# Reading places to registers per stretch instead of per group in a graph network's count stage

## The chip, the cores and the metric

The kernel runs on one core of a Trainium2 chip. Its time is device time in microseconds (us) for one launch. The unchanged kernel took 1696.02 us (median of three runs, 1693.77 to 1696.36).

A core has five engines with a queue of instructions each: PE (matrix multiply; PEld is its weight load), DVE and ACT (elementwise, vector and scalar engine), POOL (elementwise and general) and SP (here an issuer of DMAs). An engine's queue also executes instructions that compute nothing, such as a register load; in the profile such time is marked with a q (ACTq, POOLq, DVEq) and doesn't count as busy.

## What is computed

A graph has 6250 nodes with 128 features and 200,000 edges, sorted by their target `dst`; each edge has a source `src` and 128 features of its own. The reference, cut to what matters:

```python
h = relu(layernorm(x))
agg_src  = segment_sum(h[src], dst, 6250)
agg_edge = segment_sum(edge_attr, dst, 6250)
x = x + relu(concat([h, agg_src, agg_edge]) @ W.T + b)
h = relu(layernorm(x))
for Wl, bl, Wr in two layers:                      # mean over a node's edges
    agg = segment_sum(h[src], dst, 6250) / maximum(degree, 1)
    h = relu(agg @ Wl + bl + h @ Wr)
x = x + h
```

## The kernel before

**Two phases.** The sum over edges of `h[src]` is turned into a matrix product with a matrix of edge counts (how many edges go from source s to target d). The first phase, up to some 720 us of the profiled span, builds these counts in DRAM (`counts_d`) and adds up the edge features (`aggE`). The second (from L657 on) multiplies the counts with the nodes' features, once per layer (L753); the change doesn't touch it.

**Groups, tiles, windows.** The edges come in 196 groups of 1024, a group as U = 8 tiles of 128. For each group DVE writes one-hots by comparing an index with `iota`: `sp` (the source's row, 8 x 128, L567) and `sq` (target and source column within a window, L570), and weighs one of them (L572 or L574). For n = 1 a third one, `sc` (L584), carries edges over the border between windows. PE multiplies `sp` with `sq` into the PSUM tile `pu` (L597, L609; two windows per tile, three buffers). A window takes n tiles: 4 in the first 28 groups, 2 in the next 56, 1 in the last 112. ACT copies a window's counts from `pu` into an SBUF tile, the ring, at a place that depends on the data.

**The places.** `at_i` holds a window's place in the ring for every tile, `first_i` the first node of every group; both are int32 on one partition, computed on the chip. An engine that uses such a place reads it to a register first. `group_values` (L431) makes one instruction (TENSOR_LOAD, L433) that reads several values, `value` (L427) one that reads one (L428). In every group ACT reads its windows' places (L576: 2, 4 or 8 values for n = 4, 2, 1; they are n apart in `at_i`) and, for n > 1, POOL reads the same again (L578). For n = 1 ACT alone puts a window into the ring (L624). For n > 1 ACT copies the first columns, which overlap the window before, to `fore` (L619), POOL adds them to the ring (L627), and ACT puts the rest (L629).

**Stretches and rings.** Consecutive groups share one ring for a stretch: 14 groups in the first region, then 7, 4, 3, 2, and 2 or 3 for n = 1; 70 stretches in all, 44 of them with n = 1. At a stretch's end POOL reads `first_i` and issues the DMA that writes the ring to `counts_d` (L646, L647), between 0.3 and 1.8 MB by the width of its region. For n > 1 POOL begins a stretch by copying the seam from the ring before (L561, L562). There are three rings in turn, so a ring is free again when the write of three stretches earlier has landed.

**Edge features and first layer beside it.** `edge_sums` (L477) loads a group's features (512 KB, SP's queue, five buffers), has DVE write a one-hot `hot` (L484), has PE multiply (L493), and then reads the group's first node to a DVE register (L496) and adds the result into `aggE` there (L498). It is a generator: L635 lets it emit its 8 matmuls spread between those of the counts, by the shares of L546, and each is tied behind the last count matmul. Every third group also emits one block of the first layer (L641): statistics, a transpose through `pu` (L387), the product with the weights (L394), ACT's copies hT (L389) and feats (L395).

**Order.** The program's order is what the loops emit; the framework's scheduler may move an instruction ahead of earlier ones of its engine that are not ready in its own model, and the order per engine is then fixed. The one-hots `sp`, `sq` and `sc` come from the pool `hots` with two buffers each (L410); a third group's one-hots have to wait until PE has read the first's.

Of the kernel before, what the change touches and what calls it, by code (L numbers as in the profile page):

```python
# [19 lines left out]
ET = mybir.EngineType  # L20
# [5 lines left out]
U = 8  # L26
# [10 lines left out]
NONE = 2047.0  # L37
RUN = 14
XB = 4


REGIONS = (
# [20 lines left out]
def kernel(ctx: ExitStack, tc: tile.TileContext, x, srcl, dstl, edge, w0t, b0, w1l, b1, w1r, w2l, b2, w2r, out):  # L63
# [11 lines left out]
    nc = tc.nc  # L75
    N = x.shape[0]
# [3 lines left out]
    NJ = -(-NB // NC3)  # L80
    G = srcl.shape[1] // U
# [62 lines left out]
    aggE = keep.tile([P, NP + WINMAX], F32, name="aggE")  # L144
    c_early = keep.tile([P, P, NJ], I32, name="c_early")

    build = ExitStack()
# [5 lines left out]
    at_i = lists.tile([1, GC * U], I32, name="at_i")  # L153
    first_i = lists.tile([1, G], I32, name="first_i")
# [43 lines left out]
    for key, t in [*pick.items(), *pick_l.items()]:  # L198
        n = key if isinstance(key, int) else key[0]
# [110 lines left out]
    while si < NS:  # L310
        g0, k = stretches[si][:2]
# [95 lines left out]


    rings = build.enter_context(tc.tile_pool(name="rings", bufs=1))
    hots = build.enter_context(tc.tile_pool(name="hots", bufs=2))  # L410
    edges = build.enter_context(tc.tile_pool(name="edges", bufs=5))

    ring_of = [rings.tile([P, SWMAX * NJ], I32, name=f"ring{i}") for i in (2, 1)]
# [13 lines left out]
    def value(ap, engine, most):  # L427
        return nc.values_load(  # L428
            ap, engines=[engine], min_val=0, max_val=most, skip_runtime_bounds_check_because="clamped on the chip"
        )  # L430

    def group_values(ap, engine, most):
        _, values = nc.values_load_multi_w_load_instructions(  # L433
            ap, engines=[engine], min_val=0, max_val=most, skip_runtime_bounds_check_because="clamped on the chip"
        )
        return values
# [17 lines left out]
    def carries():  # L454
# [19 lines left out]
            carry[:, 0:1], flat_q[:, T1 - 2 : T1 - 1], pu[:, 0:1].unsqueeze(2).to_broadcast([P, 1, 2]), op=ALU.subtract  # L474
        )

    def edge_sums(g):  # L477

        win = win_of(g)
        e = edges.tile([P, U, D], F32, name="edge_t")  # L480
        at_e = min(g * EG, E - EG)
        nc.sync.dma_start(e, edge[at_e : at_e + EG, :].rearrange("(p u) f -> p u f", u=U))
        hot = padded[g % len(padded)]
        nc.vector.tensor_tensor(  # L484
            hot[:, : U * win].rearrange("p (u w) -> p u w", w=win),
            iota[:, :win].unsqueeze(1).to_broadcast([P, U, win]),
            rel[:, g, :].unsqueeze(2).to_broadcast([P, U, win]),
            op=ALU.is_equal,
        )
        ps = bpsum.tile([P, 512], F32, name="pe", bufs=2)  # L490
        for u in range(U):
            behind = yield
            mm = nc.tensor.matmul(ps[:, :P], e[:, u, :], hot[:, u * win : u * win + P], start=u == 0, stop=u == U - 1)  # L493
            if behind is not None:
                tc.add_manual_dep(mm.ins, behind.name, IN_ORDER, reason="in turn with the counts")
        base = value(first_i[0:1, g : g + 1], ET.DVE, N - 1)  # L496
        to = aggE[:, bass.ds(base, win)]
        nc.vector.tensor_tensor(to, to, ps[:, :win], op=ALU.add)  # L498

    def all_edge_sums():  # L500
# [54 lines left out]
    for si, (g0, ng, n, w, k, sw, win) in enumerate(stretches):  # L555
        nq = NJ * w
        ring = ring_of[si % 3]
        if si == NS - 1:
            nc.gpsimd.memset(ring[:, : sw * NJ].bitcast(F32), 0.0)
        if before is not None and n > 1:  # L560
            v = value(seam_i[0:1, si : si + 1], ET.Pool, (SWMAX - 1) * NJ)  # L561
            nc.gpsimd.tensor_copy(ring[:, :NJ], before[:, bass.ds(v, NJ)])  # L562
        for g in range(g0, g0 + ng):
            if g == RUN:
                carries()
            sp = hots.tile([P, U, P], BF16, name="sp")
            onehots(sp, p_e[:, g], U, P)  # L567
            even = nq + nq % 2
            sq = hots.tile([P, U, NQ + NQ % 2], BF16, name="sq")
            onehots(sq[:, :, :even], q_e[:, g], U, even)  # L570
            if nq < P and n > 1:
                weigh(sq[:, :, :even], g, even)  # L572
            else:
                weigh(sp, g, P)  # L574
            places = at_i[0:1, g * U : (g + 1) * U : n]
            to_put = group_values(places, ET.Activation, (sw - w) * NJ)  # L576
            if n > 1:
                to_add = group_values(places, ET.Pool, (sw - w) * NJ)  # L578
            else:

                of_first = 2 if g == G1 else 1
                sc = hots.tile([P, U + 1, NJ + NJ % 2], BF16, name="sc")
                c0 = g * U - T1 + 1
                onehots(  # L584
                    sc[:, 2 - of_first : U + 1], carry[:, c0 + 1 - of_first : c0 + U], U + of_first - 1, NJ + NJ % 2
                )
            live = [t for t in range(0, U, n) if g < G - 1 or (t + n) * P > unused]
            many = 2 if nq <= 512 else 1
            for j in range(0, len(live), many):
                units = live[j : j + many]  # L590
                pu = bpsum.tile([P, 2 * 512], F32, name="pu", bufs=3)
                for i, t0 in enumerate(units):
                    for t in range(t0, t0 + n):
                        c = i * 512
                        while c < i * 512 + nq:
                            z = min(c // 512 * 512 + 512, i * 512 + nq)
                            mm = nc.tensor.matmul(  # L597
                                pu[:, c:z],
                                sp[:, t, :],
                                sq[:, t, c - i * 512 : z - i * 512],  # L600
                                start=t == t0,
                                stop=t == t0 + n - 1 and (n > 1 or c > i * 512),
                            )
                            c = z
                    if n == 1:

                        slot = t0 + 1 if t0 != live[0] else 1
                        for j0, (sp_b, t) in enumerate(last_tiles):
                            mm = nc.tensor.matmul(  # L609
                                pu[:, i * 512 : i * 512 + NJ],  # L610
                                sp_b[:, t, :],
                                sc[:, slot + 1 - len(last_tiles) + j0, :NJ],
                                start=False,
                                stop=j0 == len(last_tiles) - 1,
                            )
                    last_tiles = [(sp, t) for t in range(t0, t0 + n)]
                if n > 1:
                    fore = hots.tile([P, 2, NJ], I32, name="fore", bufs=8)
                    nc.scalar.copy(  # L619
                        fore[:, : len(units), :], pu.rearrange("p (i c) -> p i c", c=512)[:, : len(units), :NJ]  # L620
                    )
                for i, t0 in enumerate(units):
                    if n == 1:
                        nc.scalar.copy(ring[:, bass.ds(to_put[t0], nq)], pu[:, i * 512 : i * 512 + nq])  # L624
                        continue
                    to = ring[:, bass.ds(to_add[t0 // n], NJ)]
                    add = nc.gpsimd.tensor_tensor(to, to, fore[:, i, :], op=ALU.add)  # L627
                    tc.add_to_no_dep_group(f"add{si}", add.ins)
                    put = nc.scalar.copy(  # L629
                        ring[:, bass.ds(to_put[t0 // n] + NJ, nq - NJ)], pu[:, i * 512 + NJ : i * 512 + nq]  # L630
                    )

                    tc.declare_no_dep(put.ins, group=f"add{si}", reason="a later window's other nodes stand behind it")
                spent += share(n) * len(units) / len(live)
                sum_edges(min(int(spent / shares * GU + 0.5), GU), counted)  # L635
                counted = mm.ins

            if len(writes) > 1 or block == NB and writes:
                writes.pop(0)()
            if g % 3 == 1 and block < NB:  # L640
                writes.append(first_layer(block))  # L641
                block += 1
        if si == 0:
            begin = 0
        else:
            begin = value(first_i[0:1, g0 : g0 + 1], ET.Pool, N - 1) * NJ  # L646
        write = nc.gpsimd.dma_start(counts_d[:, bass.ds(begin, sw * NJ)], ring[:, : sw * NJ])  # L647
        if si >= EARLY:
            tc.declare_no_dep(write.ins, group="early", reason="it begins behind the first block, or all is computed again")
        if si == EARLY - 1:  # L650
            tc.add_to_no_dep_group("early", load_counts(nc.gpsimd, c_early, 0).ins)
        before = ring
# [547 lines left out]
```

## Time and profile before

| | before |
|---|---|
| median of the runs shown | 1696.02 us |
| the profiled execution | 1698.32 us |
| its span | 1696.7 us |
| granted TensorE clock | 0.977 |
| PE, DVE, ACT, POOL busy | 92%, 77%, 51%, 18% |
| register loads: ACT L433, POOL L433 | 196, 84 |
| register loads: DVE L428 | 196 |
| ring writes (POOL, L647) | 70 |

The table's counts and shares come from one profiled execution. A line of a group of instructions names the source line, the engine, the operation and out<-in; a line of waits reads "who waited <- for whom: us in total, times, longest us". The chain of waits goes back from the last instruction to what released each step and gives shares by line; it can be asked for a window of time alone. The windows give each engine's busy time in a stretch of the span.

### The profile page before, as it was taken

To read this page: it belongs to the slowest core of one execution; us is meant where nothing else is said; L and a number is where in the kernel's file an instruction comes from. 1 tells how busy PE (TensorE), PEld (TensorE's weight loads), DVE (VectorE), ACT (ScalarE), POOL (GpSimd) and SP (SyncE) were. 2 spreads that over 40 slices of the span, in tenths; PEclk is the share of its full clock that TensorE was granted. 3 is DMA by queue.
4 is the path that set the end of the run, shared out by engine and by line. 5 is a ranking of instruction groups with operands and counts; after the bars stand their busy time and mean duration, and the time that the engine had idled before them with its cause. 6 is when DMAs were issued, how large, how long until landed. Compare 5 with 4: busy or idle time off the path is not lost.

```text
span 1696.7 us, 38957 instructions
## 1 busy us (share of the span) xinstructions
PE 1561.9 (92%) x13563; PEld 1506.6 (89%) x13563; DVE 1303.3 (77%) x2810; ACT 869.3 (51%) x2183; POOL 297.3 (18%) x657
## 2 busy tenths in 40 slices
PE   5998887889988888779999999899999999999998
PEld 5897777778878877669999999899999999999998
DVE  9887776678878778777777777888676777777775
ACT  3434443566766666655555555554444453444442
POOL 2534555200000000131211222201000020000000
PEclk9999998999999999979999999999999999999999
DMA  1877766678877788766666567455555556666662
GB/s 61 261 255 252 246 224 220 237 259 278 284 274 273 276 294 311 270 230 209 199 204 214 199 222 227 169 185 199 196 189 202 185 174 206 228 219 220 221 223 97
DMA packets 122572, 377.02 MB, mean 222 GB/s; under 512 B 15249, under 2 KB 67151, under 8 KB 99712
## 3 DMA queue, kind: packets, MB, share of 16 engines
q1 hardware_dynamic: 98676, 289.00, 51.2%
q0 software_dynamic: 15088, 80.80, 12.9%
q10 hardware_dynamic: 8604, 4.66, 0.9%
q8 instruction: 109, 1.79, 0.4%
q14 instruction: 95, 0.78, 0.2%
HBM read 289.94 MB, written 84.45 MB: 221 GB/s over the span
## 4 chain that ended last, share of the span: by engine, by line
PE 69%; ACT 11%; issue 7%; ACTq 4%; DVE 4%; DMA 3%; POOL 1%; POOLq 1%; DVEq 0%
PE ps L753 50%; PE pe L493 10%; ACT ring L624 9%; ACTq L433 4%; PE pu L597 3%; DMA counts_d<-ring 3%; PE pz L394 2%; PE pu L394 1%; PE pt L296 1%; PE pt L387 1%; PE ps L751 1%; ACT ring L629 0%; DVE sq L440 0%; DVE sp L440 0%; DVE w_n L247 0%
## 5 line engine op out<-in xcount | busy, mean ns | idle before, releaser
L753 PE MATMUL ps<-terms,wide 128*128 128x256 f32 (+1 forms) x7203 | 939.7, 290 | 20.0 <-DVE terms L706 13.0
L753 PEld LDWEIGHTS ps<-terms,wide 128*128 128x128 f32 x7203 | 905.5, 198 | 26.4 <-issue 13.2
L697 DVE CAST wide<-c 128x1024 fp32r<-128x1024 uint8 (+1 forms) x584 | 524.2, 907 | 145.8 <-PE ps L753 145.3
L697 ACT CAST wide<-c 128x1024 fp32r<-128x1024 uint8 x292 | 361.5, 1238 | 294.3 <-PE ps L753 233.5
L493 PE MATMUL pe<-hot,edge_t 128*128 128x128 f32 x3136 | 490.2, 293 | 8.8 <-DVE aggE L498 5.0
L493 PEld LDWEIGHTS pe<-hot,edge_t 128*128 128x128 f32 x3136 | 406.2, 196 | 15.2 <-DVE aggE L498 6.2
L624 ACT CAST ring<-pu 128x170 f32 (+6 forms) x891 | 256.1, 289 | 135.3 <-PE pu L609 57.4
L597 PE MATMUL pu<-sq,sp 128*128 128x136 bf16 (+8 forms) x1563 | 200.3, 225 | 61.5 <-ACT ring L624 37.3
L597 PEld LDWEIGHTS <-sp 128*128 128x128 bf16 x1563 | 135.6, 100 | 32.4 <-issue 25.8
L440 DVE TENSOR_TENSOR sp<-iota,p_e 128x1024 bf16<-128x1024 f16 x196 | 134.9, 688 | 37.5 <-PE pu L597 20.6
L440 DVE TENSOR_TENSOR sq<-iota,q_e 128x1088 bf16<-128x1088 f16 (+8 forms) x196 | 141.8, 723 | 13.2 <-PE pu L609 12.1
L398 POOL DMA_DIRECT2D r_d<-r x98 | 53.4, 545 | 506.4 <-DVE r L397 484.3
L609 PEld LDWEIGHTS <-sp 128*128 128x128 bf16 x892 | 80.7, 97 | 57.9 <-issue 51.6
L627 POOL TENSOR_TENSOR ring<-ring,fore 128x17 int32 x280 | 101.8, 363 | 116.0 <-ACT fore L619 37.8
L609 PE MATMUL pu<-sc,sp 128*128 128x17 bf16 x892 | 112.5, 173 | 0.0
L629 ACT CAST ring<-pu 128x119 f32 (+5 forms) x280 | 65.8, 245 | 75.8 <-issue 34.1
L647 POOL DMA_DIRECT2D counts_d<-ring x70 | 37.9, 542 | 374.5 <-ACT ring L624 310.4
L450 DVE TENSOR_TENSOR sp<-sp,w_e 128x1024 bf16<-128x1024 bf16 x140 | 95.9, 685 | 0.0
L484 DVE TENSOR_TENSOR hot<-iota,rel 128x64 f32<-128x64 f16 (+13 forms) x196 | 94.2, 484 | 0.0
L498 DVE TENSOR_TENSOR aggE<-aggE,pe 128x8 f32 (+13 forms) x196 | 37.7, 193 | 56.7 <-PE pe L493 38.2
L397 DVE TENSOR_TENSOR r<-pz,b_sb 128x128 f32<-128x128 f32 x98 | 28.0, 286 | 67.1 <-ACT feats L395 66.7
L772 DVE TENSOR_REDUCE y<-ps 128x128 f32<-128x256 f32 x147 | 60.9, 415 | 8.4 <-PE ps L753 8.4
(167 smaller groups left out, 961.1 us busy)
## 6 DMA issues: line engine op xcount, KB each, us to landing
c<-counts_d SPq DMA_DIRECT2D x146, 1088.0 KB, 5.0
edge_t<-in_edge SPq DMA_DIRECT2D x196, 512.0 KB, 4.6
own<-r_d SPq DMA_DIRECT2D x147, 64.0 KB, 1.8
counts_d<-ring POOLq DMA_DIRECT2D x5, 1785.0 KB, 7.9
counts_d<-ring POOLq DMA_DIRECT2D x5, 1598.0 KB, 8.2
counts_d<-ring POOLq DMA_DIRECT2D x5, 1462.0 KB, 8.0
counts_d<-ring POOLq DMA_DIRECT2D x5, 1377.0 KB, 6.2
r_d<-r POOLq DMA_DIRECT2D x98, 64.0 KB, 2.1
```

Of the source, the lines that this page charges most:

```text
L433: _, values = nc.values_load_multi_w_load_instructions(ap, engines=[engine], min_val=0, max_val=most, skip_runtime_bounds_check_because="c ...
L440: nc.vector.tensor_tensor(to.rearrange("p t (c two) -> p t c two", two=2), iota[:, :m].rearrange("p (c two) -> p c two", two=2).unsqueeze( ...
L450: nc.vector.tensor_tensor(pairs, pairs, w_e[:, g].bitcast(BF16).unsqueeze(2).to_broadcast([P, U, m // 2, 2]), op=ALU.mult)
L484: nc.vector.tensor_tensor(hot[:, : U * win].rearrange("p (u w) -> p u w", w=win), iota[:, :win].unsqueeze(1).to_broadcast([P, U, win]), re ...
L493: mm = nc.tensor.matmul(ps[:, :P], e[:, u, :], hot[:, u * win : u * win + P], start=u == 0, stop=u == U - 1)
L597: mm = nc.tensor.matmul(pu[:, c:z], sp[:, t, :], sq[:, t, c - i * 512 : z - i * 512], start=t == t0, stop=t == t0 + n - 1 and (n > 1 or c ...
L609: mm = nc.tensor.matmul(pu[:, i * 512 : i * 512 + NJ], sp_b[:, t, :], sc[:, slot + 1 - len(last_tiles) + j0, :NJ], start=False, stop=j0 == ...
L624: nc.scalar.copy(ring[:, bass.ds(to_put[t0], nq)], pu[:, i * 512 : i * 512 + nq])
L627: add = nc.gpsimd.tensor_tensor(to, to, fore[:, i, :], op=ALU.add)
L629: put = nc.scalar.copy(ring[:, bass.ds(to_put[t0 // n] + NJ, nq - NJ)], pu[:, i * 512 + NJ : i * 512 + nq])
L697: copy(t[:, : p1 - p0], two)
L753: dense = nc.tensor.matmul(ps[:, :m], wide[i, q][:, p, :, two], terms[:, s, :m], start=s == 0, stop=s == NB - 1)
```

## The change

The register reads are taken out of the group: ACT and POOL read all places of a stretch in its first group, in one instruction each; DVE reads the first nodes of 14 groups at once. The uses index into the longer lists. The pool `hots` gets three buffers. The diff, whole:

```diff
@@ -37,6 +37,7 @@
 NONE = 2047.0
 RUN = 14
 XB = 4
+FIRSTS = 14
@@ -407,7 +408,7 @@
-    hots = build.enter_context(tc.tile_pool(name="hots", bufs=2))
+    hots = build.enter_context(tc.tile_pool(name="hots", bufs=3))
@@ -474,6 +475,8 @@
+    bases = []
+
     def edge_sums(g):
@@ -493,8 +496,9 @@
-        base = value(first_i[0:1, g : g + 1], ET.DVE, N - 1)
-        to = aggE[:, bass.ds(base, win)]
+        if g % FIRSTS == 0:
+            bases[:] = group_values(first_i[0:1, g : min(g + FIRSTS, G)], ET.DVE, N - 1)
+        to = aggE[:, bass.ds(bases[g % FIRSTS], win)]
         nc.vector.tensor_tensor(to, to, ps[:, :win], op=ALU.add)
@@ -572,11 +576,12 @@
-            places = at_i[0:1, g * U : (g + 1) * U : n]
-            to_put = group_values(places, ET.Activation, (sw - w) * NJ)
-            if n > 1:
-                to_add = group_values(places, ET.Pool, (sw - w) * NJ)
-            else:
+            if g == g0:
+                places = at_i[0:1, g0 * U : (g0 + ng) * U : n]
+                to_put = group_values(places, ET.Activation, (sw - w) * NJ)
+                if n > 1:
+                    to_add = group_values(places, ET.Pool, (sw - w) * NJ)
+            if n == 1:
@@ -621,13 +626,13 @@
-                        nc.scalar.copy(ring[:, bass.ds(to_put[t0], nq)], pu[:, i * 512 : i * 512 + nq])
+                        nc.scalar.copy(ring[:, bass.ds(to_put[(g - g0) * U + t0], nq)], pu[:, i * 512 : i * 512 + nq])
                         continue
-                    to = ring[:, bass.ds(to_add[t0 // n], NJ)]
+                    to = ring[:, bass.ds(to_add[((g - g0) * U + t0) // n], NJ)]
...
-                        ring[:, bass.ds(to_put[t0 // n] + NJ, nq - NJ)], pu[:, i * 512 + NJ : i * 512 + nq]
+                        ring[:, bass.ds(to_put[((g - g0) * U + t0) // n] + NJ, nq - NJ)], pu[:, i * 512 + NJ : i * 512 + nq]
```

## The prediction, made before the result

> **What bounds the kernel now.** I read the page's chain first, then busy time by stage, then the chain of each stage, then every register load.
>
> ```profile
> PE 69%; ACT 11%; issue 7%; ACTq 4%; DVE 4%; DMA 3%; POOL 1%; POOLq 1%; DVEq 0%
> PE ps L753 50%; PE pe L493 10%; ACT ring L624 9%; ACTq L433 4%; PE pu L597 3%; DMA counts_d<-ring 3%; PE pz L394 2%; PE pu L394 1%; PE pt L296 1%; PE pt L387 1%; PE ps L751 1%; ACT ring L629 0%; DVE sq L440 0%; DVE sp L440 0%; DVE w_n L247 0%
> ```
>
> ACTq L433 is ACT's instruction queue standing at a register load: 4% of 1696.7 us can be touched at all. The layers (L753, from 720 us on) hold none of the edited lines. Busy time by stage (the first group takes n = 4 tiles per window until 112 us, n = 2 until 311, n = 1 until 720):
>
> ```profile
> core 0: us, PE busy (x) PEld busy (x) DVE busy (x) ACT busy (x) POOL busy (x), PEclk, DMA share, GB/s
> 44.00:112.00 68.00, 64.86 (x647) 61.87 (x645) 59.62 (x187) 26.72 (x118) 34.21 (x64) 0.95 0.82 263
> 112.00:190.00 78.00, 70.10 (x676) 64.77 (x676) 63.48 (x200) 36.05 (x198) 37.67 (x104) 1.00 0.77 253
> 190.00:311.00 121.00, 97.10 (x836) 89.52 (x835) 86.24 (x222) 48.07 (x244) 62.80 (x160) 0.92 0.68 227
> 311.00:720.00 409.00, 353.35 (x3592) 326.06 (x3592) 321.44 (x732) 267.43 (x954) 29.36 (x56) 0.98 0.79 277
> ```
>
> PE leaves 56 us idle for n = 1 and 24 us in the second half of n = 2; that is where time is to be had. The chain of those two stages, n = 1 first:
>
> ```profile
> by line: ACT ring L624 37.8%; PE pe L493 18.0%; ACTq L433 11.8%; issue 11.6%; PE pu L597 6.5%; DMA counts_d<-ring 5.5%; PE pu L394 1.5%; ACT h L376 1.2%; PE pu L609 0.9%; DVE sq L440 0.8%; ACTq L624 0.8%; DMA x_c<-in_x 0.8%; DVE sp L440 0.6
> ...
> by line: issue 31.3%; DMA counts_d<-ring 18.1%; PE pe L493 14.0%; ACTq L433 5.9%; POOLq L433 5.2%; PE pu L597 5.0%; POOL ring L627 4.5%; ACT ring L629 3.7%; POOLq L428 3.5%; POOLq L627 2.6%; ACT fore L619 1.7%; PE pu L394 1.0%; POOLq L647 0
> ```
>
> For n = 1, ACT's loads are 11.8% of 409 us = 48 us of the chain. PE's waits agree:
>
> ```profile
> PE pu L597 <- ACT ring L624: 37.3, 64, 2.4
> PE pe L493 <- DVE aggE L498: 5.0, 6, 2.4
> ```
>
> In the second half of n = 2, POOL has no room. One stretch of it:
>
> ```profile
> 240.39 0.56 POOL L647 DMA_DIRECT2D counts_d<-ring  x1 [0.80 <-ACT ring L629]
> 240.95 0.73 POOL L562 COPY ring<-ring 128x17 int32 x1
> 242.71 1.42 POOL L627 TENSOR_TENSOR ring<-ring,fore 128x17 int32 x4 [1.03 <-issue]
> 244.92 1.93 POOL L627 TENSOR_TENSOR ring<-ring,fore 128x17 int32 x4 [0.79 <-ACT ring L629]
> 247.35 0.56 POOL L647 DMA_DIRECT2D counts_d<-ring  x1 [0.49 <-ACT ring L629]
> ```
>
> The 1.03 and the 0.79 are the tails of at_i loads (1.62 and 1.08 us); the rest of the 7 us is POOL's own work.
>
> **What a load costs.** Durations are minimum/median/maximum in ns: windows 80-98 us (two values, 4 apart), 190-305 us (four values, 2 apart), 340-720 us (eight in a row).
>
> ```profile
> L433 POOLq TENSOR_LOAD <-at_i x7: 495/497/502, 81.3 to 95.9; - x7
> L433 ACTq TENSOR_LOAD <-at_i x7: 472/475/666, 82.6 to 96.8; - x7
> ...
> L433 ACTq TENSOR_LOAD <-at_i x31: 882/899/2895, 190.1 to 302.3; - x31
> L433 POOLq TENSOR_LOAD <-at_i x31: 940/1162/2540, 193.1 to 303.9; - x31
> ...
> L433 ACTq TENSOR_LOAD <-at_i x103: 537/550/2937, 342.2 to 714.0; - x103
> ```
>
> Values that lie apart cost ACT (0.888-0.471)/2 = 0.21 us each over 0.055 fixed, POOL 0.22 over 0.05: batching them saves almost nothing. Eight in a row cost 0.55, hence 0.49 over the same fixed part. The maxima matter more. Put beside the issues of ring writes (L647), load by load, slow ones begin about 1 to 3.5 us after an issue: DVE's one-value load takes 0.30 outside, 0.7 to 1.6 inside; ACT's eight take 0.55 and mostly 1.7 to 2.5. Each stretch has one such slow load in its middle or second group; at 573 us a write is issued, at 575.5 ACT's load takes 2.26, and 1.96 of that is on the chain.
>
> **The change, part by part.** ACT, n = 1 (112 groups in 24 stretches of three and 20 of two). The 110 loads that start there add up to 112.7 us; unslowed they would be 110 x 0.55 = 60. After it: 24 values in a row cost between 1.1 (one value 0.30, each further one (0.55-0.30)/7) and 3 x 0.55 = 1.65; I take 0.055 + 3 x 0.49 = 1.53, nearest to the row of eight, and 1.04 for 16. Sum 24 x 1.53 + 20 x 1.04 = 58 us. They stand at the stretch's start. There, in 30 of the 44, ACT now loads from 0.3 us before its last put ends; POOL issues 0.3 after that end; so 1.53 us end 0.9 after the issue, just short of the slow time. In the other 14 first-layer work comes first and part of the load falls into it. The slow eight lose 1.6 over two halves, 0.8 a step; I add a quarter of a step to the 30 and one and a half to the 14, 23 us. So 81 replaces 113: -32 of load time. Of the 113, 48 were on the chain (0.43 per us): -14. Each load is also followed by some 0.2 us until the next put, against 0.03 between puts; 66 loads fewer x 0.18 x 0.43 = -5. Together **-19**, between -5 and -45 (all of the chain's 48 less a little). Queued behind the longer load are the puts of L624 and hT and feats of the first layer; PE waits for them, but has three pu buffers of some 0.73 us (two windows and their edge matmuls) ahead, which hide 1.5 us. Where that cover is gone each load costs its 1.2 us.
>
> One rule speaks against this: the Trainium skill (Perfetto Trace Analysis, Identifying the Most-Contended Engine) calls the engine with the highest occupancy the one to optimize, and takes ScalarE's occupancy as a fair measure. ACT is busy 267 of 409 us, PE 353: by the rule ACT has 35% to spare and its loads are worth 0, the whole change +12 from POOL and DVE below, 1708. The row ACTq L433 says 48 us, because a load holds ACT's queue without counting as busy. I follow the row.
>
> POOL, n = 2. In 190-311 us 16 stretches have 32 loads, 44.8 us: the first, issued 0.4 us after the ring write, averages 1.76, the second 1.04. One load of eight values then costs at least 1.83 unslowed plus the first's present excess, 2.6; at most twice the slowest seen, 5.1. I take 2 x 1.76 = 3.5, each half slowed like the first now: +0.7 per stretch. Some 0.25 of the second load lay under POOL's last add and is now exposed; one handover less gives 0.15 back. +0.8 x 16 x 0.8 (POOL waits for ACT about a fifth of this stage) = **+10** (0 to +25). Behind it stand the adds (L627), the next ring write and so, over the ring's reuse, ACT's puts. In 112-190 us nine longer stretches by the same 0.8, at half weight since PE is 90% busy: **+4** (0 to +10). A second rule would price this otherwise: Runtime: NRT & Kernel Launch, breakdown of the preamble, gives a TENSOR_LOAD some 1.3 us as one round trip to HBM for a few words. Per instruction, POOL would gain 16 x 1.3; but these loads read SBUF, and the rows go by value, two 0.50, four 0.94. I take the rows.
>
> ACT, n = 2: 112 values apart in 112-190 us are 24 us plus slowing, about 30, against 28.8 now: 0 (-6 to +6); there is slack, for ACT runs ahead of POOL. n = 4: one load of 28 values (5.9 us on ACT, 6.3 on POOL) at 45-53 us, before ACT's first count is there at 55; then 3.0 us twice, under three pu buffers of about 2 us each: 0 (to +4).
>
> DVE: 196 loads, 101 us, become 14 loads of 14 values, from 0.9 (by the row of eight) to 4.3 (one by one); I take 0.9. The aggE add and the one-hots behind it queue after it. PE waited for that add only 5.0 us: **-2** (-5 to +4).
>
> Third one-hot buffer: DVE waits 25 us for PE to free sp or sq for n = 1 and 18 for n = 2, but PE hardly ever waits for one-hots, so DVE was merely early: 0; down to -5, or up to +5 if one-hots are now put ahead of aggE adds.
>
> Sum: -19 + 10 + 4 - 2 = -7 on an execution of 1698.3 us (span 1696.7 and 1.6 around it), 1691 there. That execution lies 2.3 above the median of 1696.0, so on the median **1689**.
>
> **Rivals.** *POOL hidden, ACT fully freed:* the n = 1 chain loses nearly all 48 us, POOL's extra is absorbed: 1696 - 40 = 1656. For it: PE's idle 56 us; against: POOL has no gaps in n = 2. *Loads are priced by value wherever they stand* (the batch doesn't save what it says): POOL's +14 and -14 on ACT and DVE: 1696. For it: two and four apart are proportional. *Slower: the ring write catches ACT's batch.* If ACT's load of 24 starts over 0.1 us later relative to the issue, as in the 14 stretches now, it runs through the slow time; three steps at +0.8 give 1.5 + 2.3 = 3.9 against 3.2 for three loads before, of which 0.6 more was hidden: with the handovers +0.9 per stretch of three, +0.8 of two, 38 us, about half on the chain, +20, and POOL's +14: 1730. Against it: 30 of 44 stretches start their load in time.
>
> **Numbers.** Likeliest case 0.50, own range 1676 to 1696; all freed 0.16; cancelled 0.12; slower 0.22, from 1700 to 1735. The range, 1658 to 1712, leaves out the fastest part of the second and the slowest of the fourth. A measurement can tell about 0.2%, 3.4 us, that is below 1692.6 or above 1699.4: faster 0.41 + 0.16 = 0.57, same 0.09 + 0.09 = 0.18, slower 0.03 + 0.22 = 0.25.
>
> **What would show it.** ACT loads for n = 1: 44, mean 1.5 to 2.1; ACTq L433 at some 7% of that stage and its length about 390; POOL loads above 3 us and 190-311 longer by about 10. I am wrong if ACT's batches exceed 2.5 us, if POOL's stay under 2.6, or if PE waits for DVE's adds.

## The result and the profile after

The changed kernel took 1720.97 us (median of four runs, 1715.31 to 1725.43) against 1695.9 for the one before (four runs beside it): ratio 1.0149, interval 1.0113 to 1.0184. The forecast was 1689, with a range of 1658 to 1712. The change is slower by 25 us.

In the profiled execution (span 1723.8 us) the layers start 24.4 us later than before (753.1 against 728.7) and then take 970.7 us against 968.0. So nearly all of the loss lies in the count phase. The page's chain after, by engine and by line:

```profile
PE 70%; issue 9%; DVE 5%; ACT 5%; ACTq 4%; DMA 3%; POOLq 1%; POOL 1%; DVEq 0%
PE ps L758 49%; PE pe L496 12%; ACTq L434 4%; ACT ring L629 3%; PE pu L602 3%; DMA counts_d<-ring 3%; PE pz L395 2%; DVE sp L441 1%; PE pt L297 1%; PE pu L395 1%; PE pt L388 1%; DVE sq L441 1%; ACT ring L634 1%; PE ps L756 1%; POOLq L434 1%
```

ACTq still has 4% though its reads fell from 196 to 70: fewer reads, as much time on the chain. L434 is now the read of several values on every engine. To compare stages I cut them where the last ring write of a stage is issued: n = 4, the n = 2 stretches of four and three groups, the n = 2 stretches of two groups, n = 1. Before, they took 71.2, 94.5, 105.9 and 404.4 us. The windows of the first two stages before, and of all four after:

```profile
44.00:115.20 71.20, 68.06 (x682) 65.03 (x680) 62.21 (x195) 28.61 (x126) 34.64 (x66) 0.95 0.81 261
115.20:209.70 94.50, 81.45 (x779) 75.20 (x778) 74.96 (x233) 40.84 (x227) 47.19 (x131) 0.99 0.76 252
...
44.00:134.10 90.10, 75.59 (x707) 70.62 (x704) 63.98 (x221) 28.10 (x138) 33.92 (x67) 0.90 0.64 216
134.10:249.90 115.80, 88.63 (x708) 79.65 (x706) 69.12 (x199) 35.68 (x202) 42.71 (x130) 0.89 0.54 184
249.90:361.60 111.70, 86.94 (x776) 81.33 (x775) 76.90 (x197) 47.92 (x229) 52.76 (x140) 0.95 0.67 228
361.60:744.40 382.80, 346.58 (x3566) 324.84 (x3565) 313.57 (x724) 266.46 (x942) 27.21 (x48) 0.98 0.82 293
```

The columns are as in the prediction. The stages changed by +18.9, +21.3, +5.8 and -21.6. A stage's length from a single execution wavers: in runs that left all reads of a stage as they were, n = 4 took 71.2 to 73.4 us, the longer n = 2 stretches 92.5 to 96.1, and n = 1 took 392.5 to 404.4. So the first two losses are far outside the noise, and the gain for n = 1 is somewhere between 10 and 22 us. The loss is in the two stages that I had put at 0 and +4, and it shows twice: PE is idle longer, and it is slower when busy (together 164.2 us busy with 1415 matmuls, where 149.5 us had served for 1461; granted clock 0.90 and 0.89 against 0.95 and 0.99). One place shows how. The timeline of PE at the start of the first seven-group stretch:

```profile
89.38 1.01 PE L465 MATMUL pu<-steps,ones 1*128 1x448 f32 x2
90.33 0.53 PE L602 MATMUL pu<-sq,sp 128*128 128x102 bf16 x8
90.69 0.45 PE L496 MATMUL pe<-hot,edge_t 128*128 128x128 f32 x2
90.98 0.52 PE L602 MATMUL pu<-sq,sp 128*128 128x102 bf16 x8
91.34 0.67 PE L496 MATMUL pe<-hot,edge_t 128*128 128x128 f32 x4
94.78 0.52 PE L602 MATMUL pu<-sq,sp 128*128 128x102 bf16 x8 [2.76 <-ACT ring L634]
95.13 2.28 PE L496 MATMUL pe<-hot,edge_t 128*128 128x128 f32 x10
...
108.03 1.34 PE L496 MATMUL pe<-hot,edge_t 128*128 128x128 f32 x10
```

and ACT's in the same time:

```profile
90.95 0.19 ACT L624 CAST fore<-pu 128x34 int32<-128x34 f32 x1 [3.26 <-PE pu L602]
94.23 0.49 ACT L634 CAST ring<-pu 128x85 f32 x2 [3.09 <-issue]
```

ACT's batch (14 values, 3.1 us) stands in its queue behind the copy to fore, which waits for PE's first windows. So ACT idles 3.26 us without reading, and then reads for 3.1 while PE waits. The three pu buffers hold a part of the carry (L465) and two groups' windows (eight matmuls each); with only six edge matmuls among them PE filled these two within 1.2 us, and then stood for 2.76. The ten edge matmuls after that took 2.28 us, where ten took 1.34 at 108 us: the clock had fallen. Windows of 2 us around it (the third column from the end is the granted clock):

```profile
90.00:92.00 2.00, 2.00 (x24) 1.51 (x23) 1.57 (x4) 0.19 (x1) 0.21 (x1) 1.00 0.03 8
92.00:94.00 2.00, 0.02 (x1) 0.00 (x0) 0.26 (x1) 0.00 (x0) 0.00 (x0) 1.00 0.91 279
94.00:96.00 2.00, 1.23 (x13) 1.22 (x13) 1.14 (x4) 0.91 (x5) 1.18 (x3) 0.83 0.70 276
96.00:98.00 2.00, 2.00 (x11) 2.00 (x11) 0.83 (x2) 0.34 (x3) 0.28 (x1) 0.50 0.01 2
98.00:100.00 2.00, 2.00 (x20) 1.85 (x18) 1.08 (x4) 1.10 (x6) 0.44 (x2) 0.82 0.02 6
```

The half clock lasted from 95.3 to 98.7 us. Over n = 4 and the longer n = 2 stretches PE's gaps (over 0.1 us) grew from 16.1 to 41.1 us, and the time at half clock from 9.0 to 44.4, of which I take half as lost: 25.0 + 17.7 = 42.7 us, against the 40.2 by which these two stages grew. This is an estimate: part of the half clock fell into gaps, and 46 matmuls that these stages did before come later in the changed kernel.

### The profile page after: what moved, and what is told of

It is laid out like the page before. It is cut to its first block, busy times and chain, and to the rows that moved or that the text cites. A ratio compares the mean times of both kernels' runs of the same rounds, so it can differ in the third digit from the quotient of the medians.

```text
span 1723.8 us, 38611 instructions
## 1 busy us (share of the span) xinstructions
PE 1576.0 (91%) x13563; PEld 1522.5 (88%) x13563; DVE 1294.8 (75%) x2810; ACT 869.2 (50%) x2183; POOL 289.8 (17%) x657
## 4 chain that ended last, share of the span: by engine, by line
PE 70%; issue 9%; DVE 5%; ACT 5%; ACTq 4%; DMA 3%; POOLq 1%; POOL 1%; DVEq 0%
PE ps L758 49%; PE pe L496 12%; ACTq L434 4%; ACT ring L629 3%; PE pu L602 3%; DMA counts_d<-ring 3%; PE pz L395 2%; DVE sp L441 1%; PE pt L297 1%; PE pu L395 1%; PE pt L388 1%; DVE sq L441 1%; ACT ring L634 1%; PE ps L756 1%; POOLq L434 1%
## 5 line engine op out<-in xcount | busy, mean ns | idle before, releaser
L496 PE MATMUL pe<-hot,edge_t 128*128 128x128 f32 x3136 | 505.2, 298 | 14.6 <-DVE aggE L502 7.8
L496 PEld LDWEIGHTS pe<-hot,edge_t 128*128 128x128 f32 x3136 | 420.2, 201 | 22.3 <-DVE aggE L502 10.7
L629 ACT CAST ring<-pu 128x170 f32 (+6 forms) x891 | 257.7, 289 | 116.1 <-PE pu L614 59.9
L632 POOL TENSOR_TENSOR ring<-ring,fore 128x17 int32 x280 | 94.0, 336 | 168.7 <-ACT ring L634 83.5
L614 PEld LDWEIGHTS <-sp 128*128 128x128 bf16 x892 | 80.9, 97 | 40.2 <-issue 34.8
L634 ACT CAST ring<-pu 128x68 f32 (+5 forms) x280 | 65.7, 244 | 68.2 <-issue 63.6
L487 DVE TENSOR_TENSOR hot<-iota,rel 128x64 f32<-128x64 f16 (+13 forms) x196 | 94.2, 481 | 0.0
L624 ACT CAST fore<-pu 128x34 int32<-128x34 f32 x140 | 26.8, 191 | 90.5 <-PE pu L602 54.0
```

Of the source, the lines that this page charges most:

```text
L487: nc.vector.tensor_tensor(hot[:, : U * win].rearrange("p (u w) -> p u w", w=win), iota[:, :win].unsqueeze(1).to_broadcast([P, U, win]), re ...
L614: mm = nc.tensor.matmul(pu[:, i * 512 : i * 512 + NJ], sp_b[:, t, :], sc[:, slot + 1 - len(last_tiles) + j0, :NJ], start=False, stop=j0 == ...
L629: nc.scalar.copy(ring[:, bass.ds(to_put[(g - g0) * U + t0], nq)], pu[:, i * 512 : i * 512 + nq])
L634: put = nc.scalar.copy(ring[:, bass.ds(to_put[((g - g0) * U + t0) // n] + NJ, nq - NJ)], pu[:, i * 512 + NJ : i * 512 + nq])
```

## Experiments

All kernels but those named "change" start from the kernel before; times are medians, beside runs of the kernel before on the same chip. Differences in us are the ratio's, of 1697; the ratio isn't the quotient of the two medians, and the medians alone would differ from it by up to 4 us (expectations written between the runs use them). Stage lengths come from one execution each. My theory before the first run: ACT's long batches for n = 4 and 2 stop PE, and its clock falls. Rivals: the third one-hot buffer, and POOL's batches.

**The third buffer alone.**

```diff
-    hots = build.enter_context(tc.tile_pool(name="hots", bufs=2))
+    hots = build.enter_context(tc.tile_pool(name="hots", bufs=3))
```

> The kernel before with three one-hot buffers and every register read left in its group. Theory 1 (the loss comes from ACT's long batched reads in the n = 4 and n = 2 stretches, which stop PE and let its clock fall; n = 1 gains about 21 us): about 1696, within 4. Rival 2 (the third buffer lets the scheduler order DVE worse, and that is the loss): the n = 4 and n = 2 stages grow by 20 or more, total 1710 or more.

1695.9 against 1697.2, ratio 0.9995 (0.9982 to 1.0008): alone it does nothing that is measured.

**The change with two buffers** (the same line set back in the changed kernel).

> The changed kernel's batched reads on ACT, POOL and DVE with two one-hot buffers. Theory 1: about 1720 as the changed kernel, n = 4 and n = 2 longer by about 45, n = 1 shorter by about 20. Rival 2 (buffers): n = 4 and n = 2 as before, total about 1675.

1732.5, ratio 1.0211 (1.0181 to 1.0241). Not the buffer's fault: with two it is 11 us worse. So the third buffer gains under batches; that it covers some of the stops that they make is the likely reason, and isn't shown.

**ACT's batches for n = 1 alone.** A variable sets how many groups one read serves:

```diff
-            to_put = group_values(places, ET.Activation, (sw - w) * NJ)
+            per = ng if n == 1 else 1
+            if (g - g0) % per == 0:
+                to_put = group_values(
+                    at_i[0:1, g * U : min(g + per, g0 + ng) * U : n], ET.Activation, (sw - w) * NJ
+                )
...
```

> Only ACT's reads for n = 1 are batched per stretch; everything else as before. Theory 1: n = 1 takes about 383 us in place of 404, the stages before it unchanged: 1675. If the gain for n = 1 came from DVE's reads or the third buffer: about 1696.

1670.6, ratio 0.9867 (0.9835 to 0.9898), and n = 1 took 375.4 us, 29 less than in the profile before and 17 less than the shortest that this stage took unchanged; the ratio makes it 23. ACT's reads there fell from 110 of 1.02 us on average to these (minimum/median/maximum in ns):

```profile
L433 ACTq TENSOR_LOAD <-at_i x42: 1012/1490/3357, 318.6 to 681.5; - x42
```

A median of 1.49, for 24 values, is the 1.53 of the prediction; the batch mostly does end ahead of the slow time beside the ring write (7 of the 42 took over 1.6 us). This part seems to gain more than the whole change does for n = 1 (375.4 against 382.8), which points to something else in it that loses there.

**The batches for n = 4 and n = 2 alone** (`per = 1 if n == 1 else ng`, and the same for POOL).

> Only the reads for n = 4 and n = 2 are batched, on ACT and POOL; n = 1, DVE and the buffers as before. Theory 1: ACT's batches of 3 to 6 us stop PE for over 2 us per long stretch and its clock is granted at half for 3.4 us after each: n = 4 about +19, n = 2 about +27, total about 1740. Rival 2: 1696 to 1702. Rival 3 (POOL's reads alone): +14, 1710, with no loss of clock.

1723.1, ratio 1.0170 (1.0142 to 1.0198), +29 us, less than the 43 expected. Then each engine's half of it:

> Of the batches for n = 4 and n = 2 only ACT's; POOL reads in every group. Batching both cost 26 us. Theory 1 (ACT's long read keeps PE waiting for a pu buffer): most of it, 1712 to 1722, with ACT's reads of 3 us and more ahead of PE's gaps. Rival 3 (POOL's reads): 1697 or less.

ACT alone: 1708.0, ratio 1.0054 (1.0037 to 1.0071), +9.

> Of the batches for n = 4 and n = 2 only POOL's; ACT reads in every group. Theory 1: 1700 to 1708, the 4 to 10 us that POOL's later adds cost where POOL is full. Rival 3: 1715 or more. If both halves of the change are needed for the loss (POOL late and ACT late together): both single runs under 1705.

POOL alone: 1712.8, ratio 1.0084 (1.0063 to 1.0104), +14. My theory, that most of it is ACT's, did not hold: both results lie outside what it expected, POOL's share is no smaller than ACT's, and the two make up most of the loss (23 of 29). In the run with ACT's alone n = 4 took 80.4 us and the long n = 2 stretches 100.3, with POOL's alone 77.2 and 98.1, against 71.2 and 94.5; the two-group stretches took 105.0 with ACT's, 109.6 with POOL's, 105.9 before.

**DVE's batches alone.** What was left over in the sum pointed to them:

```diff
-        base = value(first_i[0:1, g : g + 1], ET.DVE, N - 1)
-        to = aggE[:, bass.ds(base, win)]
+        if g % 14 == 0:
+            bases[:] = group_values(first_i[0:1, g : min(g + 14, G)], ET.DVE, N - 1)
+        to = aggE[:, bass.ds(bases[g % 14], win)]
```

> Only DVE's reads are batched, 14 first nodes at a time. The prediction put -2 on this: 1694. What is left when the runs with ACT for n = 1 (-26) and with ACT and POOL for n = 4 and 2 (+26) are taken from the changed kernel (+24) and from it with two buffers (+35) says the opposite: about +20 or more, 1715 to 1725, if the parts add up. In the changed kernel these reads take 1.3 us where the first of the 14 stands at a multiple of four, 3.2 us where it doesn't, and 5.5 and 6.7 us beside a ring write.

1715.1, ratio 1.0098 (1.0077 to 1.0119): +17 from 14 instructions. The parts, each measured with two one-hot buffers, are -23 (ACT, n = 1), +29 and +17: +23. The change with two buffers measured +36, so together they lose some 13 us more than one by one; the third buffer takes 11 of this back, and so the sum comes out near the +25 of the change by luck. Three of the batches, one by one:

```profile
L433 DVEq TENSOR_LOAD <-first_i x1: 1315/1315/1315, 314.5 to 314.5; - x1
...
L433 DVEq TENSOR_LOAD <-first_i x1: 5385/5385/5385, 367.9 to 367.9; - x1
...
L433 DVEq TENSOR_LOAD <-first_i x1: 8021/8021/8021, 679.4 to 679.4; - x1
```

The timeline of DVE and POOL at the last of them:

```profile
680.74 0.23 DVE L440 TENSOR_TENSOR sc<-iota,carry 128x144 bf16<-128x144 f16 x1
687.57 0.23 DVE L501 TENSOR_TENSOR aggE<-aggE,pe 128x74 f32 x1 [6.61 <-issue]
687.72 0.77 DVE L486 TENSOR_TENSOR hot<-iota,rel 128x592 f32<-128x592 f16 x1
...
679.53 0.53 POOL L657 DMA_DIRECT2D counts_d<-ring  x1 [0.42 <-ACT ring L634]
```

POOL issues a ring write 0.2 us after the read begins; the read of 14 values then takes 8 us, the next edge one-hot stands behind it on DVE, and PE waited 6.2 us for that one-hot. PE's waits for DVE from 317 to 740 us in this run:

```profile
PE pu L607 <- DVE sp L450: 9.7, 3, 3.8
PE pe L495 <- DVE hot L486: 7.5, 5, 6.2
PE pe L495 <- DVE aggE L501: 4.3, 4, 2.8
```

That is 21.5 us for one-hots and adds, where the kernel before had 5.5 for n = 1 (5.0, 0.3 and 0.2): about the loss.

**Values in a row.** For n = 4 and 2 the chip writes the places side by side, and a group's read takes two or four neighbours; ACT's batches for n = 1 as above, all else as before:

```diff
-    nc.vector.tensor_scalar(at_i, flat(room), 0.0, float(NJ), op0=ALU.max, op1=ALU.mult)
...
+    for g0, g1, n in runs:
+        count = (g1 - g0) * U // n
+        place0[n] = filled - g0 * U // n
+        nc.vector.tensor_scalar(
+            at_i[:, filled : filled + count], flat(room)[:, g0 * U : g1 * U : n], 0.0, float(NJ), op0=ALU.max, op1=ALU.mult
+        )
+        filled += count
...
```

> ACT's reads for n = 1 batched as in the third run, and the places for n = 4 and n = 2 written to at_i side by side, so that a group's two or four values are in a row; still read in every group. If a read is priced by runs of four values and not by value: ACT's and POOL's reads of four fall from 0.89 and 0.94 us to about 0.35, POOL gets 28 x 2 x 0.6 us back in the two-group stretches: n = 2 about 15 us shorter, total about 1655. If the price is by value: 1671, as the third run.

1660.5, ratio 0.9758 (0.9737 to 0.9780). The reads of four values between 200 and 300 us:

```profile
L442 ACTq TENSOR_LOAD <-at_i x30: 307/312/2108, 202.5 to 299.3; - x30
L442 POOLq TENSOR_LOAD <-at_i x28: 313/320/1124, 200.4 to 298.3; - x28
```

0.31 and 0.32 us, where values two apart took 0.90 and 1.16 at the median. Four neighbours cost what one value costs (DVE's 0.30 to 0.31). The n = 2 stages took 190.2 us together, 10 less than in the kernel before and 6 less than in the third run; I had expected 15.

**The same, and batched per stretch.**

> The eighth run with the reads for n = 4 and n = 2 batched per stretch as well (ACT and POOL), now out of places side by side. A batch then takes about 0.6 (8 values), 1.0 (16) and up to 1.8 us (28) where the changed kernel took 1.7, 3.4 and 6.1. If the loss of batching for n = 4 and 2 (+29) came from the length of these reads, this is within 8 of the eighth run, 1655 to 1668. If it came from their standing at the stretch's start whatever their length: 1680 or more.

1669.4, ratio 0.9840 (0.9811 to 0.9870): just above the first expectation's range (1668), far from the second's (1680), and 0.8% above the run without batches. In the profiles the two-group stretches became 9 us shorter by these batches (101.4 to 92.3), and n = 4 and the longer n = 2 stretches 18 us longer.

**DVE's batches from multiples of four** (16 in place of 14).

> Only DVE's reads batched, 16 first nodes at a time, so that every batch begins at a multiple of four values. Unslowed reads should take about 1.4 us throughout, none 3.2. If the odd batches' reading by value is what costs 17 us (14 at a time, 1715): 1695 to 1702. If a batch of any kind on DVE, at the wrong moment beside a ring write, is what costs: 1705 or more.

1700.1, ratio 1.0015 (0.9999 to 1.0031): of +1.0% little or nothing is left. The reads:

```profile
L433 DVEq TENSOR_LOAD <-first_i x13: 947/1220/3079, 50.9 to 697.5; - x13
```

It wasn't that these batches met no ring write: five of the 13 began 0.6 to 3.0 us after one was issued, and took 1.7 to 3.1 us.

**Values in a row with three buffers.**

> The eighth run with three one-hot buffers. Alone the third buffer changed nothing (0.9995), but with all batches it was worth 11 us (1732 to 1721). If it helps only where reads stop an engine for long: 1660 as the eighth run, within 4. If it helps wherever ACT no longer sets the pace: about 1652.

1651.8, ratio 0.9732 (0.9708 to 0.9755), 45 us faster than before and the fastest so far. The eighth run's median was 1660.5, but on another chip, on which the kernel before took 1700.4 against 1697.5 here; the intervals of the two ratios overlap, so that the third buffer helps here is not shown. The n = 1 stage, in the fastest execution of this run (1645.6):

```profile
302.60:665.60 363.00, 338.24 (x3571) 317.75 (x3569) 313.40 (x724) 266.77 (x943) 27.16 (x47) 1.00 0.86 311
```

PE is busy for 338 of 363 us, at full clock.

**The change, mended:** all its batches and buffers, with places side by side and DVE's batches of 16.

> The whole change (batches on ACT, POOL and DVE, three one-hot buffers) with places side by side and DVE's batches of 16. If the price by value of reads that lie apart or begin off a multiple of four explains the loss: 1655 to 1670. If batches at a stretch's start cost of themselves: 1690 or more.

1662.0, ratio 0.9798 (0.9764 to 0.9832). As expected: the whole change gains 2% once its reads are short. Against the run before (1651.8), it still lost 10 us; two more runs asked where.

> The eleventh run (places side by side, ACT's n = 1 reads per stretch, three buffers) with ACT's and POOL's n = 2 reads batched where a stretch has two groups. If only the long stretches lose by batching: n = 2 in two-group stretches 5 to 9 us shorter, total 1643 to 1650. If a batch at the start costs of itself: 1655 or more.

1653.9, ratio 0.9752 (0.9697 to 0.9807).

> All reads of ACT and POOL batched, places side by side, three buffers, DVE in every group. If the long stretches' batches are what is left of the loss: 1660, slower than the run beside it by 10 or more, the seven-group stretches longest, where one read of 14 values begins off a multiple of four and takes over 3 us. If DVE's batches of 16 made the twelfth run slow: as the run beside it, within 4.

1652.5, ratio 0.9732 (0.9677 to 0.9787). Neither differs from 0.9732 by more than its interval. So with three buffers short batches on ACT and POOL bring and cost nothing, within 0.55%, over per-group reads in a row; in the profiles the two-group stretches gain by them (98.1 to 85.8 us) what n = 4 and the longer n = 2 stretches lose (160.5 to 169.8). The twelfth run's difference points to DVE's batches, which that run alone has besides: its n = 4 stage took 88.1 us, against 75.2 in the fourteenth run. But the intervals overlap (0.9764 to 0.9832 and 0.9677 to 0.9787), and the cause stays open.

## Why the prediction was wrong

- **ACT and DVE for n = 1 (-19 and -2):** measured -21.6 in the profiles, and that this is the forecast's -21 is luck: it is the sum of two larger parts. ACT's alone are -23 by the ratio (-29 in the profiles, 404.4 to 375.4), inside the range given; the batch's price (1.53, measured 1.49) and, mostly, its place ahead of the slow time held. DVE's batches alone lengthened the stage, 404.4 to 419.6.
- **The third buffer (0):** right, 0.9995. That it is worth 11 us under batches was not foreseen.
- **POOL, two-group stretches (+10):** sign right, +5.8 in the changed kernel, +3.7 in the run with POOL's batches alone, both inside the range; a read took 3.0 us at the median where I took 3.5.
- **The first failed step:** "then 3.0 us twice, under three pu buffers of about 2 us each: 0 (to +4)", and for n = 2 "there is slack, for ACT runs ahead of POOL". The price of the read was right (3.1 us). Its cover was not: the buffers are shared with the carry and the first layer, PE fills two in 1.2 us where few edge matmuls stand between, and the read stands behind a copy that itself waits for PE. n = 4 lost 18.9 us, the longer n = 2 stretches 21.3 where I had +4; PE's waits for ACT's puts (L629 before, L634 after) rose from 8.4 to 20.3 us in these stages. Of this loss POOL's part is no smaller than ACT's (alone +14 against +9). How POOL's reads reach PE is shown only in part.
- **What no step contained:** the price of a stop for PE's clock. I counted a stop at its length. Here gaps of 2.23 and 2.76 us were followed by half clock for 3.4 us each. By my sum 25 us of gaps cost 25; by the clock row about 18 more. The Trainium skill (TensorE: Matmul & The Clock Gate, Part 1) has the clock fall to half after an idle window of about 3.4 us; these gaps are shorter, and the measurement decides. In the two profiles half clock begins and ends on a grid of 3.41 us; from 44 us on all 30 full-clock windows of it in which PE was busy under half of the time (by the profile's records) were followed by half clock, and none of those with over 55%. So a gap of 1.7 us was enough at 577 us in the kernel before.
- **Also in no step:** DVE's order at the start. The first edge one-hot (L487) came at 51.6 us in place of 48.3, and PE waited 3.0 us for it. The same stop, 3.0 to 3.5 us, stands in four more runs that batch POOL's reads for n = 4, POOL's alone among them, and in none that leaves these per group. Why the framework puts it there was not tried.
- **The second failed step:** "DVE: ... I take 0.9", by the row of eight values. Half of the batches of 14 begin off a multiple of four values and took 3.2 us; those of them beside a ring write took 5.4 to 8.0. I had both facts for ACT (values apart cost each; slow time beside a write) and didn't apply them to DVE. It was +17 alone, against a range of -5 to +4, with PE's added waits mostly for the one-hots that queue behind the read.
- **The slower rival** (ACT's batch of 24 caught by the ring write, 1730) had nearly the right total by the wrong place: the median batch for n = 1 is 1.49 us. The chance that I gave to slower was 0.25, and 0.22 of it was this rival's.
- **Against occupancy** the row was right: ACT, busy 65% for n = 1, was worth 23 us (0.9867) by a change to its reads alone. With the reads counted in, ACT was taken 344 of 409 us in the profile before (267 busy and 113 reading, in part at once), almost as much as PE (353). That the rule's total, 1708, came nearer to the result than mine is luck: it had no loss on n = 4 either.

## What to carry to other kernels

Fewer register reads are not shorter ones: put the values side by side, begin at a multiple of four, and keep a batch short or where its engine has nothing else due; a longer read in an in-order queue is a stop for everything behind it. Before calling a stop hidden, count the buffers that are really free at that point, and ask what the stop costs the engine that waits, its clock included. And take a change of several parts apart, and don't expect the parts to add: -23, +29 and +17 were all in this one, and the version without the two losses is 2.7% faster than the kernel before.

## What the runs showed of the hardware

A read of several registers took about 0.05 us plus 0.21 to 0.22 for each value that stands apart; two values side by side were no cheaper (0.49 against 0.47), four from a multiple of four took 0.31 together, sixteen 1.02 to 1.10, and fourteen 1.32 when they begin at a multiple of four, 3.2 when not. In the microseconds after a large ring write was issued such reads were slower: one value mostly 0.7 to 1.7 us in place of 0.30, fourteen up to 8.0. That the write itself slows them is likely, but was not tested. PE's granted clock stood at half for 3.4 us or a multiple after a window of 3.41 us in which PE was busy less than about half of the time, and gaps of 2.2 us, at times 1.7, were enough for it; by the estimate that half of the time at half clock is lost, a stop of 2.8 us cost some 4.5.
